# A macaron block on one core: the L1 mixtures in two per pass, one a sequence, with attention's key sums on TensorE and the RWKV set-up moved down

## The chip, the cores and the metric

The kernel runs on one core of one Trainium2 chip. The metric is device time in microseconds (us); lower is better. All arithmetic is in f32. The kernel before ran three times: 1630.42, 1637.78 and 1638.27 us, median 1637.78 us.

## The reference, cut to what matters

The input is two sequences of 1024 tokens with 256 features, 2048 tokens in all. Six residual steps follow each other, three of "layer 0" and three of "layer 1":

```
x = x + 0.5 * moe0(layernorm(x))      # 8 experts, the best 2 per token, hidden 176, and a shared part
x = x + rwkv(layernorm(x))            # a token needs the token before it
x = x + 0.5 * moe0(layernorm(x))      # same weights
x = x + 0.5 * moe1(layernorm(x))      # 32 experts, the best 6 per token, hidden 96, and a shared part
x = x + attention(layernorm(x))
x = x + 0.5 * moe1(layernorm(x))      # same weights
```

A mixture routes each token by a softmax (layer 0) or a sigmoid (layer 1) over its experts and adds the weighted outputs of `silu(x Wg) * (x Wu) Wd` of the chosen experts. The shared part is one more such network that all tokens go through. Nothing in a mixture ties one token to another.

The attention of layer 1 is linear. It works on one sequence:

```
Q, K, V = split(X @ W_in.T + b_in);   Q, K = rope(Q), rope(K)     # first 128 features turned
A = sum over tokens of (K / max(|K|, 1e-12)) * V                  # one vector of 256 per sequence
Y = (A * Q) @ W_out.T + b_out + X
```

So a token's output needs all tokens of its own sequence, and none of the other's.

## The kernel before, in words

**Tiles.** All of x stays in SBUF, as 16 tiles of 128 tokens; tiles 0 to 7 are the first sequence, 8 to 15 the second. The code calls eight tiles a half (`HT`), and four tiles a batch (`BT`).

**A mixture (`sparse_moe`, L311).** Its steps are generators, one for each of these:

- `ready(h)` (L674) for a half: `prep` (L339) normalizes a batch on VectorE, transposes it on TensorE (L123), multiplies it with the router (L354) and picks the experts (`route`, L133). `plan` (L377) ranks the tokens of each expert with three matmuls (L390 to L397) and gives every pair of token and expert a slot. Slots lie in blocks of 128, and a block belongs to one expert. `owners` (L469) lists each block's expert.
- `scatter(h)` (L450): GpSimd writes each normalized row to its slots in a DRAM buffer `xs`, with one indirect DMA for a tile and one choice: 16 for a half of layer 0, 48 for a half of layer 1.
- `shared(h)` (L542): the shared network, a tile at a time.
- `blocks()` (L656): for each block, SP fetches 128 slots (`fetch`, L569), TensorE transposes them (`features`, L580), multiplies with gate and up weights (`inner`, L593), ScalarE and VectorE form silu times up (L503, L504), TensorE turns that and multiplies it with the down weight (`outward`, L608), VectorE copies it out (L616), and SP stores it to a DRAM buffer `ys`. The four steps of neighbouring blocks are taken in turn, one of each per round. A fetch waits for all scatters issued so far.
- `combine(h)` (L645): GpSimd gathers each pair's row from `ys` (L627), VectorE adds it, weighted, to x (L638), four gathers behind.

The number of blocks is fixed beforehand, for the worst split of tokens over experts (`moe_blocks`, L40): 39 for layer 0 and 127 for layer 1. Slots of layer 1's second half that fit into blocks of the first are put there. A gather for the first half waits for the first 79 blocks (23 in layer 0), one for the second half for all blocks.

**The order of the work.** `play` and `side_by_side` (L272 to L308) run the generators beside each other. Each yields an engine and an assumed time; the one whose planned clock is lowest goes next. What comes out is a fixed order of instructions for TensorE, VectorE, ScalarE and SP (`ORDERED`). Each of these engines takes its instructions in that order and stands when one has to wait. GpSimd's order is set by the framework's own scheduler. `after` (L1014) holds a generator until named steps have been planned.

**The stages.** Loads of x, of layer 0's weights and a fill of `xs` with zeros open SP's queue; the ten small RWKV vectors and seven RWKV weights follow (`load_rwkv`, L700). There, five small VectorE operations form one minus a mixing vector (L708); they are the first that VectorE has to do after three set-up operations. Then come the first layer-0 mixture over all 16 tiles, RWKV in four batches, the second layer-0 mixture, the first layer-1 mixture over all 16 tiles, attention of the first sequence, routing of its tiles for the second layer-1 mixture, attention of the second sequence (`attend`, L869), routing, and the second layer-1 mixture over all 16 tiles, whose results are stored.

**Attention.** For each tile (`products`, L890) TensorE forms queries, keys and values, VectorE adds biases and turns queries and keys. In `sums` (L931) ScalarE squares the keys and sums them, VectorE adds the residual and the bias, takes the root's reciprocal for that tile, multiplies key, value and that number (L947) and adds it to an accumulator (L948). Two matmuls with a column of ones at the end sum over the partitions. `queries` (L950) transposes the queries. After the last tile the output weight is scaled by A, and the output matmuls follow.

Of the kernel before, what the change touches and what calls it, by code (L numbers as in the profile page):

```python
# [8 lines left out]
F32 = mybir.dt.float32  # L9
I32 = mybir.dt.int32  # L10
# [29 lines left out]
def moe_blocks(m):  # L40
    return (NTOK * m["K"] + m["E"] * (P - 1)) // P
# [3 lines left out]
def macaron_kernel(ctx: ExitStack, tc: tile.TileContext, a: dict, out: bass.AP):  # L45
# [58 lines left out]
    def normalize(src, dst, n, name):  # L104
# [9 lines left out]
        for i in range(n):  # L114
            nc.vector.tensor_scalar(  # L115
                dst[i], src[i], mv[:, i, 0:1], rstd[:, i : i + 1], ALU.subtract, ALU.mult
            )

# [68 lines left out]
    def sparse_tiles(pool, layer):  # L187
# [17 lines left out]
            blocks=moe_blocks(m),  # L205
# [49 lines left out]

    def fill_slots(xs, n, behind=None):

        zero = const.tile([P, D], F32, tag="zero", name=f"zero_{n}")
        nc.gpsimd.memset(zero, 0.0)
# [12 lines left out]
    def side_by_side(*parts):  # L272

        clocks, waits = [clock["now"]] * len(parts), [None] * len(parts)
        left = set(range(len(parts)))
        while left:
# [9 lines left out]
            n = min(able, key=lambda n: (clocks[n], n))  # L286
            if clocks[n] > clock["now"]:
                yield "until", clocks[n]
# [15 lines left out]
    def play(*parts):  # L304
        for step in side_by_side(*parts):
# [5 lines left out]
    def sparse_moe(layer, w, nth, xs, ys, moe, last=False):  # L311

        name = f"{layer}_{nth}"
        E, K, H, C, HP, NBLK = (w[k] for k in ("E", "K", "H", "C", "HP", "blocks"))
        SH, SU, rows = w["SH"], w["SU"], w["rows"]

        first = (HT * P * K + E * (P - 1)) // P
        xs, ys = xs[0 : NBLK * P, :], ys[0 : NBLK * P, :]
# [3 lines left out]
        def begin(h):  # L322
            nonlocal taken, comb, past, slot, top, idx, wk, who, ends
            if h == 0:
                taken = moe.tile([P, NT, E], F32, tag="taken", name=f"taken_{name}")
                comb = moe.tile([P, NT, E], F32, tag="comb", name=f"comb_{name}")
                past = moe.tile([P, NT + 1, E], F32, tag="past", name=f"past_{name}")
                slot = moe.tile([P, NT, E], F32, tag="slot", name=f"slot_{name}")
                top = back.tile([P, NT, 8], F32, tag="top", name=f"top_{name}")
                idx = back.tile([P, NT, K], I32, tag="idx", name=f"idx_{name}")  # L330
                wk = back.tile([P, NT, K], F32, tag="wk", name=f"wk_{name}")
                who = moe.tile([P, P], I32, tag="who", name=f"who_{name}", bufs=2)
                ends = moe.tile([P, 2, E], F32, tag="ends", name=f"ends_{name}")
# [5 lines left out]
        def prep(b):  # L339
# [4 lines left out]
            normalize(x[ts], xb, BT, sub)  # L344
# [850 lines left out]
```

## Time and profile before

| what | value |
|---|---|
| median of three runs | 1637.78 us |
| the profiled execution's own time | 1638.15 us |
| its span, first to last instruction | 1636.0 us |
| mean granted TensorE clock | 0.868 of full speed |
| TensorE busy | 1189.7 us, 73% |
| VectorE busy | 802.1 us, 49% |
| ScalarE busy | 559.6 us, 34% |
| GpSimd busy | 523.1 us, 32% |
| DMA | 203.06 MB, mean 124 GB/s |

Stages by the timeline, from the span's start: the first transposes of a mixture at 56.8 us, the first blocks of layer 0 at 158.5, RWKV's first transposes at 268.1 and its end at 490, layer 0's second blocks from 597.5 to 709.5, layer 1's blocks from 862 to 1069 and from 1347.9 to 1564. In the profile PE is TensorE, DVE VectorE, ACT ScalarE, POOL GpSimd and SP SyncE; a name such as `xb_L<-xs_L` is what an instruction writes and reads, with numbers left out. A waiting engine is listed with what ended the wait. Every matmul in f32 counts as two records, a transpose as one. The time of a TensorE record includes its way through the array, so neighbouring records overlap, and pace is read from the starts.

### The profile page before, as it was taken

The numbers are of one execution on the slowest core, as the hardware profiler recorded it, in microseconds if no ns is written. First come the engines' busy times: TensorE is split into PE (matmuls) and PEld (weight loads), VectorE is DVE, ScalarE is ACT, GpSimd is POOL, SyncE is SP. The second block draws the span as 40 slices with busy tenths as digits, with TensorE's granted clock in tenths as the row PEclk, the third lists the DMA queues.
The fourth block names the chain that finished last, engine by engine and source line by source line (L and its number), as shares of the span: only waits on it lengthen the run. The fifth ranks groups of instructions, "written<-read, shape, count | busy, mean of one in ns | idle before, by whom it ended". The sixth has DMA issues, their size and how long they took to land.

```text
span 1636.0 us, 21526 instructions
## 1 busy us (share of the span) xinstructions
PE 1189.7 (73%) x5462; PEld 888.9 (54%) x5462; DVE 802.1 (49%) x2588; ACT 559.6 (34%) x1551; POOL 523.1 (32%) x559
## 2 busy tenths in 40 slices
PE   0489997699996999876508998964685609998820
PEld 0366764366565777644307887743454408887610
DVE  0453346855515522556503445688776514445543
ACT  0142344576723333322104554420341104453310
POOL 0042034011113400337770005556271460005556
PEclk9999998799996999976758999987696759999965
DMA  9411343920008113464225557722020135557743
GB/s 276 119 58 63 100 143 93 331 77 1 0 0 210 56 56 107 133 169 140 103 103 151 172 174 224 237 88 81 32 103 26 62 106 158 172 172 217 226 120 105
DMA packets 182911, 203.06 MB, mean 124 GB/s; under 512 B 40044, under 2 KB 165772, under 8 KB 182796
## 3 DMA queue, kind: packets, MB, share of 16 engines
q1 hardware_dynamic: 158220, 134.55, 27.6%
q0 software_dynamic: 24576, 67.14, 13.3%
q8 instruction: 52, 0.85, 0.2%
q14 instruction: 63, 0.52, 0.1%
HBM read 100.68 MB, written 100.93 MB: 123 GB/s over the span
## 4 chain that ended last, share of the span: by engine, by line
PE 44%; DVE 13%; POOL 9%; DMA 8%; issue 7%; ACT 3%; POOLq 0%; ACTq 0%; DVEq 0%; SPq 0%
PE pg_L_b L593 12%; POOL xs_L L455 8%; PE py_L_b L608 7%; PE px_L L580 4%; DMA xb_L<-xs_L 4%; PE pkv_cm L761 3%; PE pkk_cm L749 3%; DMA yk_L<-ys_L,idx_L 3%; PE pg_L L513 3%; PE ph_L_b L529 2%; PE py_L L555 2%; DVE x L638 1%; PE lg_L L354 1%; PE po_at L761 1%; POOL yk_L L627 1%
## 5 line engine op out<-in xcount | busy, mean ns | idle before, releaser
L627 POOL DMA_INDIRECT yk_L<-ys_L,idx_L x256 | 248.8, 972 | 631.1 <-DMA ys_L<-yb_L 484.2
L455 POOL DMA_INDIRECT xs_L<-xn_L,idx_L x256 | 248.2, 970 | 263.4 <-DVE idx_L L446 77.7
L504 DVE TENSOR_TENSOR h_L_b<-g_L_b,pg_L_b 128x96 f32<-128x96 f32 (+1 forms) x332 | 90.6, 273 | 370.9 <-ACT g_L_b L503 370.4
L593 PE MATMUL pg_L_b<-L1gu,xbT_L 128*128 x1016 | 220.2, 341 | 21.0 <-ACT xbT_L L584 12.9
L584 ACT COPY xbT_L<-px_L 128x256 f32<-128x256 f32 x332 | 123.5, 373 | 279.0 <-PE px_L L580 276.8
L580 PE MATMUL px_L<-ident,xb_L 128*128 128x128 f32 x664 | 130.1, 278 | 108.6 <-DMA xb_L<-xs_L 108.2
L593 PEld LDWEIGHTS pg_L_b<-L1gu,xbT_L 128*128 128x128 f32 x1016 | 163.9, 195 | 36.0 <-issue 17.6
L580 PEld LDWEIGHTS px_L<-ident,xb_L 128*128 128x128 f32 x664 | 92.1, 143 | 151.0 <-DMA xb_L<-xs_L 97.9
L638 DVE SCALAR_TENSOR_TENSOR x<-yk_L,wk_L,x 128x256 f32<-128x256 f32 x256 | 121.3, 480 | 75.1 <-DMA yk_L<-ys_L,idx_L 73.5
L616 DVE COPY yb_L<-py_L_b 128x256 f32<-128x256 f32 x332 | 140.6, 424 | 29.4 <-PE py_L_b L608 27.3
L608 PE MATMUL py_L_b<-L1down,hT_L_b 96*128 x508 | 153.4, 383 | 0.2 <-ACT hT_L_b L536 0.2
L503 ACT ACTIVATE g_L_b<-pg_L_b 128x96 f32<-128x96 f32 (+1 forms) x332 | 88.6, 267 | 160.5 <-PE pg_L_b L593 159.4
L593 PE MATMUL pg_L_b<-L0gu,xbT_L 128*128 x312 | 107.0, 466 | 6.3 <-ACT xbT_L L584 5.5
L529 PE MATMUL ph_L_b<-ident,h_L_b 128*96 128x128 f32 (+1 forms) x410 | 100.3, 276 | 2.4 <-DVE h_L_b L504 2.2
L536 ACT COPY hT_L_b<-ph_L_b 96x128 f32<-96x128 f32 (+1 forms) x332 | 92.8, 280 | 3.6 <-PE ph_L_b L529 3.5
L513 PE MATMUL pg_L<-L0sgu,xTs_L 128*128 128x352 f32 x256 | 88.9, 497 | 0.0
L608 PEld LDWEIGHTS py_L_b<-L1down,hT_L_b 96*128 96x128 f32 x508 | 77.4, 193 | 10.3 <-ACT hT_L_b L536 0.9
L608 PE MATMUL py_L_b<-L0down,hT_L_b 88*128 x312 | 81.4, 384 | 1.0 <-ACT hT_L_b L536 1.0
L503 ACT ACTIVATE g_L<-pg_L 128x176 f32<-128x176 f32 (+1 forms) x96 | 29.8, 322 | 150.4 <-PE pg_L L513 150.2
L123 PE MATMUL pt_L<-ident,xn_L 128*128 128x128 f32 x128 | 28.6, 376 | 69.6 <-DVE xn_L L115 66.7
L504 DVE TENSOR_TENSOR h_L<-g_L,pg_L 128x176 f32<-128x176 f32 (+1 forms) x96 | 31.7, 341 | 72.1 <-ACT g_L L503 72.0
L593 PEld LDWEIGHTS pg_L_b<-L0gu,xbT_L 128*128 128x128 f32 x312 | 53.6, 191 | 24.3 <-ACT xbT_L L584 6.2
(216 smaller groups left out, 1823.0 us busy)
## 6 DMA issues: line engine op xcount, KB each, us to landing
xb_L<-xs_L SPq DMA_DIRECT2D x332, 128.0 KB
ys_L<-yb_L SPq DMA_DIRECT2D x332, 128.0 KB
xs_L<-zero SPq DMA_DIRECT2D x1, 16256.0 KB
xs_L<-zero SPq DMA_DIRECT2D x1, 4992.0 KB
xs_L<-xn_L,idx_L POOLq DMA_INDIRECT x256, 2.4
yk_L<-ys_L,idx_L POOLq DMA_INDIRECT x256, 3.1
L1gu<-in_L_gate SPq DMA_DIRECT2D x8, 384.0 KB
L1gu<-in_L_up SPq DMA_DIRECT2D x8, 384.0 KB
```

Of the source, the lines that this page charges most:

```text
L455: d = nc.gpsimd.indirect_dma_start(out=xs, out_offset=bass.IndirectOffsetOnAxis(ap=idx[:, t, k : k + 1], axis=0), in_=xn[h][:, i, :], in_o ...
L503: nc.scalar.activation(g, pg[:, 0:width], AF.Silu)
L504: nc.vector.tensor_tensor(dst, g, pg[:, width : 2 * width], ALU.mult)
L513: nc.tensor.matmul(pg, xT[half][:, c, i * P : (i + 1) * P], w["sgu"][:, c, u, :, :].rearrange("p z w -> p (z w)"), start=(c == 0), stop=(c ...
L529: nc.tensor.transpose(pt[0:m, k * P : (k + 1) * P], h[:, r : r + m], ident)
L580: nc.tensor.transpose(px[:, c * P : (c + 1) * P], xb[:, c * P : (c + 1) * P], ident)
L584: nc.scalar.copy(xbT.rearrange("p c t -> p (c t)"), px[:, 0 : DC * P])
L593: nc.tensor.matmul(pg, xbT[:, c, :], w["gu"][:, c, bass.ds(e, 1), :, :].rearrange("p e z h -> p (e z h)"), start=(c == 0), stop=(c == DC - 1),
L608: nc.tensor.matmul(py, hT[0:HP, k, :], w["down"][:, bass.ds(e, 1), k, :].rearrange("p e d -> p (e d)"), start=(k == 0), stop=(k == C - 1),)
L616: nc.vector.tensor_copy(yb, py)
L627: d = nc.gpsimd.indirect_dma_start(out=yk, out_offset=None, in_=ys[0 : n * P, :], in_offset=bass.IndirectOffsetOnAxis(ap=idx[:, t, k : k + ...
L638: added = nc.vector.scalar_tensor_tensor(x[t], gathered.pop((t, k)), wk[:, t, k : k + 1], x[t], ALU.mult, ALU.add)
```

## The change

**Mixtures of layer 1.** Each of the two passes is now two mixtures, one for each sequence, called A and B. Each has its own `xs` and `ys`, its own slots and its own 79 blocks (`moe_blocks(w, HT)`). Layer 0 stays one mixture over 16 tiles. The tiles with routing data get two buffers, and `zero` is set once.

**Order.** `prep` can wait for its batch (`behind`). The first pass plans A's scatter, blocks of A with B's routing and shared network among them, then blocks of B with A's gathers and the first sequence's attention among them. The second pass does the same, with A's blocks beside B's gathers and the second sequence's attention. A filler may be named in `play`: it goes on where the others would leave TensorE free for more than 0.5 us by the plan. The second shared pass of layer 0, and that of the last mixture, are fillers. The planned costs of some steps are new numbers.

**Attention.** Residual and bias go into one operation per tile in `norms`; the norm's root is taken once for all tiles; key times value stays in the tile of normalized features, and 16 matmuls with the column of reciprocal norms form A. Scratch data is put into PSUM banks.

**Set-up.** The five RWKV operations move from the head into `rest_of_mixing`, behind the first mixture.

```diff
-def moe_blocks(m):
-    return (NTOK * m["K"] + m["E"] * (P - 1)) // P
+def moe_blocks(m, tiles=NT):
+    return (tiles * P * m["K"] + m["E"] * (P - 1)) // P
...
+        parts = [*parts, *([filler] if filler is not None else [])]
...
+            if filler is not None and len(parts) - 1 in able:
+                others = [m for m in able if m != len(parts) - 1]
+                if others:
+                    n = min(others, key=lambda n: (clocks[n], n))
+                    if clocks[n] > max(free["PE"], clocks[-1]) + 0.5:
+                        n = len(parts) - 1
...
+    def sparse_moe(layer, w, name, first_tile, tiles, xs, ys, moe, last=False, behind=None):
...
+        NBLK = moe_blocks(w, tiles)
+        halves = tiles // HT
...
+            if behind is not None:
+                yield lambda: behind(b)
...
             if "_m" in v:
-                u = pool.tile([P, DC], F32, name=f"u_{v}")
-                nc.vector.tensor_scalar(u, t, -1.0, 1.0, ALU.mult, ALU.add)
-                rw[f"1-{v}"] = u
+                rw[f"1-{v}"] = pool.tile([P, DC], F32, name=f"u_{v}")
...
+    def rest_of_mixing():
+        for v in ("tm_mk", "tm_mv", "tm_mr", "cm_mk", "cm_mr"):
+            nc.vector.tensor_scalar(rw[f"1-{v}"], rw[v], -1.0, 1.0, ALU.mult, ALU.add)
...
+            minus[g] = small.tile([P, BT], F32, tag="minus", name=f"minus_{name}_{g}", bufs=4)
+            nc.vector.scalar_tensor_tensor(minus[g], mean, -1.0, rstd, ALU.mult, ALU.mult)
+            nc.vector.tensor_scalar(rstd, rstd, 1.0, None, ALU.add)
+            for i, xt in enumerate(xs[ts]):
+                nc.vector.scalar_tensor_tensor(
+                    xt, xt, rstd[:, i : i + 1], at["b_out"], ALU.mult, ALU.add
+                )
...
-            nc.vector.tensor_tensor(xs[t], xs[t], xl[:, t, :], ALU.add)
-            nc.vector.tensor_tensor(xs[t], xs[t], at["b_out"], ALU.add)
...
-                nc.vector.scalar_tensor_tensor(v, qk[:, 1, :], ss, v, ALU.mult, ALU.mult)
-                nc.vector.tensor_tensor(acc, acc, v, ALU.add)
...
+            nc.scalar.activation(
+                pv[:, D : 2 * D], qk[:, 1, :], AF.Square, accum_out=ss[:, t : t + 1]
+            )
+            nc.vector.tensor_tensor(v, v, qk[:, 1, :], ALU.mult)
...
+            for t in range(TPB):
+                nc.tensor.matmul(
+                    pA[:, c : c + 1],
+                    xl[:, t, c * P : (c + 1) * P],
+                    ss[:, t : t + 1],
+                    start=(t == 0),
+                    stop=(t == TPB - 1),
+                )
...
+                play(*mixture(m), filler=after([(d, "ready1")], m["shared"](1)))
+                rest_of_mixing()
...
+            after([(d1[0], "ready0")], m1[0]["scatter"](0)),
+            after([(d1[0], "scatter0"), (d0, "blocks")], m0["combine"](1)),
...
+            halfs_blocks(m1[0], [(d1[0], "shared0"), (d0, "blocks")]),
...
+            halfs_blocks(m1[1], [(d1[0], "nearly")]),
+
+            after([(d1[0], "first")], m1[0]["combine"](0)),
+            after([(d1[0], "first"), (d1[1], "shared0")], attention(0)),
+            after([(at, ("done", 0, 0))], m2[0]["ready"](0)),
+            after([(d2[0], "ready0"), (d1[0], "combine0")], m2[0]["scatter"](0)),
...
+            halfs_blocks(m2[0], [(d1[1], "nearly"), (d2[0], "shared0")]),
+            after([(d1[1], "first"), (d2[0], "scatter0")], m1[1]["combine"](0)),
+            after([(d1[1], "first"), (d2[0], "shared0")], attention(1)),
+            after([(at, ("done", 1, 0))], m2[1]["ready"](0)),
+            after([(d2[1], "ready0"), (d1[1], "combine0")], m2[1]["scatter"](0)),
+            halfs_blocks(m2[1], [(d2[0], "nearly")]),
+            after([(d2[0], "first"), (d2[1], "scatter0")], m2[0]["combine"](0)),
+            after([(d2[1], "blocks"), (d2[0], "combine0")], m2[1]["combine"](0)),
+            filler=fill(
+                after([(d0, "ready1")], m0["shared"](1)),
+                after([(d2[1], "ready0")], m2[1]["shared"](0)),
+            ),
```

## The prediction

> **What bounds the kernel now.** I cut the span into stages at points read from the timeline, then read the busy time of each engine in each stage; columns are the stretch, its length, busy us (records) per engine, granted TensorE clock, DMA share, GB/s.
>
> ```profile
> core 0: us, PE busy (x) PEld busy (x) DVE busy (x) ACT busy (x) POOL busy (x), PEclk, DMA share, GB/s
> 0.00:56.80 56.80, 0.00 (x0) 0.00 (x0) 4.07 (x19) 1.58 (x2) 2.06 (x15) 1.00 0.90 252
> ...
> 709.50:861.00 151.50, 63.22 (x223) 43.92 (x222) 64.92 (x241) 17.63 (x43) 108.42 (x112) 0.64 0.45 137
> 861.00:988.00 127.00, 120.78 (x726) 105.36 (x727) 53.42 (x158) 62.65 (x243) 0.00 (x0) 0.97 0.56 168
> 988.00:1069.00 81.00, 73.13 (x419) 59.24 (x417) 50.41 (x143) 36.73 (x140) 46.54 (x48) 1.00 0.77 226
> 1069.00:1174.60 105.60, 60.01 (x194) 39.48 (x194) 85.94 (x287) 16.01 (x49) 47.43 (x48) 0.74 0.22 63
> 1174.60:1347.00 172.40, 89.61 (x340) 62.56 (x340) 92.51 (x314) 38.43 (x90) 93.68 (x96) 0.72 0.21 74
> 1347.00:1474.00 127.00, 121.31 (x728) 105.05 (x728) 53.99 (x160) 62.84 (x244) 0.00 (x0) 0.98 0.56 168
> 1474.00:1564.00 90.00, 76.64 (x413) 62.31 (x413) 49.40 (x140) 35.62 (x138) 45.59 (x48) 0.94 0.71 212
> 1564.00:1636.00 72.00, 0.70 (x2) 0.30 (x2) 24.79 (x52) 0.03 (x1) 45.42 (x48) 0.53 0.39 110
> ```
>
> In the stages of L1 blocks (861 to 1069, 1347 to 1564) TensorE is busy 85% to 96%: it bounds them. Elsewhere another thing does. From 709.5 to 861 GpSimd is busy 108 of 151 us: its indirect row moves (248.8 us for 256 gathers, 248.2 for 256 scatters, one each 1.265 us by the starts below). From 1069 to 1347, attention and the second routing, TensorE is busy 150 of 278 us at a clock of 0.72 to 0.74. The last 72 us are gathers alone.
>
> The waits, longest first (engine, tile, line, releaser: total, times, longest):
>
> ```profile
> PE px_L L580 <- DMA xb_L<-xs_L: 108.2, 19, 55.1
> ...
> DVE u_tm_mk L708 <- DMA v_tm_mk<-in_tm_mk: 48.2, 1, 48.2
> ...
> POOL zero L259 <- DMA xs_L<-zero: 28.0, 1, 28.0
> ```
>
> VectorE stands 48.2 us before its first real work, for a vector of the RWKV set-up queued behind all L0 weights. TensorE waits twice, 55.1 us the longest, for the first slots of a pass.
>
> The timeline of GpSimd before the second L1 pass:
>
> ```profile
> 1283.56 0.96 POOL L455 DMA_INDIRECT xs_L<-xn_L,idx_L  x1 [47.21 <-DVE passed_L L472]
> ...
> 1343.19 0.96 POOL L455 DMA_INDIRECT xs_L<-xn_L,idx_L  x1 [0.30 <-issue]
> ```
>
> 48 scatters take 60.9 us; the last lands 2.4 us later, and the first transposes of the blocks start at 1347.85. From that pass's ranking on TensorE (1274.4) to its first block: 73 us.
>
> TensorE where L1's normalization already stands among L0's blocks:
>
> ```profile
> 685.39 0.38 PE L580 MATMUL px_L<-ident,xb_L 128*128 128x128 f32 x2
> ...
> 690.79 2.72 PE L593 MATMUL pg_L_b<-L0gu,xbT_L 128*128 x4 [5.02 <-ACT xbT_L L584]
> ```
>
> The blocks halt 5.0 us behind a ScalarE copy, which stood behind a Sqrt that waited for VectorE.
>
> **The change, part by part.** Times are on the trace's clock. The profiled execution was 1638.15 us around a span of 1636.0; the median is 1637.78, so I add 2 us at the end. For places I use the order in which the changed program's instructions stand on each engine.
>
> *Start.* The five set-up operations leave the head of VectorE's queue; they go behind the mixture, where 5 x 0.17 us cost 1 us. The loads moved no place in SP's queue. By 10.5 us the DMA has moved 2.1 MB (estimate from its rate there, 182 to 301 GB/s), which is the first eight x tiles plus router and shared weights. Normalizing tiles 4 to 7 started at 57.6 and the first scatter at 79.45, 21.9 us later; from 10, that is 32. The zero fill ended by 30.35 (GpSimd waited for it until then), so it holds nothing. Gain 47; if loads come late, 30.
>
> *L0 mixtures.* The second shared pass is now a filler: 69 of the 160 matmuls stand behind the blocks, 6.9 tiles x 4.0 us (pace at 567 to 591) = 27.6. First mixture: second plan 35 us after the first scatter (before: 39, one tile more ahead of it), 16 scatters 20.2, landing and fetch 4.5: blocks at 92 instead of 158.5. Then +27.6 behind them: 39 us ahead. RWKV's start gap of 7.7 us shrinks to about 4, and its adds find their rows landed (2 us): 44 ahead when RWKV ends. Second mixture: the same move makes scatters (573 + 2.4), not shared work (595), set the blocks' start: 22.5 earlier, 66.5 in all. Its deferred shared work now stands under the next wait.
>
> *First L1 block.* Before, 96 scatters of both sequences had to land; now 48. L0's blocks end at 643; slots are ready about 13 us later; on GpSimd eight gathers stand ahead of the scatters and wait for L0's last store, and from the blocks' end to the first scatter it was 16.5 us (709.5 to 726), so 660; 48 scatters 60.7; landing and fetch 4.5: 725 instead of 861. TensorE's 24 + 19 us of shared work fit in the wait. The two fills write 20.7 MB instead of 16.6, some 12 us more at 331 GB/s, in the RWKV stage, where the DMA then idles from 360 to 480: nothing; 12 without that cover. **136 us ahead**; bounds 115 and 150.
>
> *More blocks.* A pass had 127 blocks, now 79 + 79: 62 more in all. A clean pass of 79 with filling took 127 us (861 to 988; 1.53 a block after filling), so they cost about 95 us, and none lies beside a wait, for TensorE bounds there.
>
> *What moves among the blocks.* By TensorE's pace at full clock: a shared pass 8 x 2.38 = 19 us (732.2 to 734.6); 16 transposes at 0.11 (a block's two take 0.22), router 2 x 1.8 (699.5 to 701.3), ranking 1.7, in all 7; attention 8 x (1.72 + 0.86 products, 4 x 0.11 transposes, 0.87 output) + 32 records of the sums at 0.11, in all 35. The sums take the place of two ones-matmuls a sequence. On VectorE a tile's burst is now 0.68 + 0.41 + 0.57 + 3 x 0.43 = 2.95, with 0.44 in the normalization; it was 4.58 in all. That saving lies under TensorE, which bounds, so it is worth nothing by itself.
>
> VectorE and ScalarE are in order, so each such burst holds block work behind it, and then TensorE. The row: from the transposes at 685.39 to the next at 695.72 is 10.3 us, less 0.9 of other transposes, against 2.5 for such a block: two normalizations cost 7 us; L1's shorter blocks have less slack: 8. A routing blocks VectorE 6.2 us (698.8 to 705.0), of which its matmuls and a block cover 4: 2 each. The plan is 7 us on VectorE, 4 uncovered; slot weights 2. Attention's normalization is 6.7 us (four more operations of 0.44), 5 uncovered, twice. An attention tile has no row inside blocks: from 0 (its 2.6 us of matmuls cover the burst) to 4; I take 0.75, as the two nearly match; the tail 3. So 18 us of halts in the first mixed stage, and 13 + 10 + 6 + 3 = 32 in each with an attention; bounds 5 and 30, 8 and 65.
>
> Here a rule speaks against the change. The row: a table load takes 1.28 us, and the Silu after the load at 690.76 starts at 692.05, with nothing between. The Trainium skill (ScalarE: Activation LUTs, What ACT_TABLE_LOAD costs) adds a drain of about 1.38 us to every switch. The order has 6, 14 and 14 loads inside the three mixed stages. By the row they are in my halts; by the rule 34 x 1.38 = 47 us more, an estimate. I take the row.
>
> *Gathers beside blocks.* 48 blocks beside 48 gathers took 81 us, and 90 where output stores joined, against 73.4 clean: +8 a stage, +15 in the last. A scatter beside blocks is not seen; from 0 to 12, I take 3, since it brings no adds.
>
> *L1 in sequence.* First sequence: 127 + 19 + 7 + 18 + 3 = 174, to 899. Second sequence with attention 0: 79 x 1.53 = 121, less 5 because diluted fetches wait less (1.42 us pace at 1060 to 1064), + 8 + 35 + 7 + 32 = 198, to 1097. Second pass, first sequence: its ranking stands behind all but the last of those 79 blocks, since all of attention precedes it, and SP's fetches wait for its scatters: **73 us in which only 19 us of shared work is left**, to 1170. Blocks with attention 1: 127 - 5 + 8 + 35 + 7 + 32 = 204, to 1374. Again 73, less 3 for two blocks behind the ranking: 1444. Blocks: 127 + 15 = 142, to 1586. Gathers of all 48 rows: 72, to 1658. Before, this part took 775 us; now 933.
>
> Against each other: 136 ahead at the front, 158 behind after it: **+22 us, 1658 + 2 = 1660**.
>
> **Rivals.**
> *Smooth interleaving (faster).* Bursts hide fully, gathers cost nothing and diluted blocks run at 1.42: mixed stages of 156, 154 and 160 us: 106 less, 1554. It decides once the three together fall more than 30 us below my 576. For it: VectorE has some 145 us of work in about 200. Against: the halt above, and gathers that cost 8 to 17.
> *VectorE paces the mixed stages.* Tiles with adds (6 us of VectorE beside 6 of TensorE) and PSUM banks held through the rotation cost 4 us a tile: +26 in each of two stages, and 10 for longer normalizations: 1722.
> *The start is not gained.* Fill, loads and scatters collide: 17 us lost, 1677.
> *Clock.* Work that ran at 0.72 should run at 1.00. The Trainium skill (TensorE: Matmul & The Clock Gate, What's actually happening) has idle of some 3.4 us halve the clock. If halts keep it at the 0.72 row, attention's 35 us become 49 a sequence: 1688. I take full clock: dense stages show 0.97 to 1.00.
>
> **How the numbers follow.** Forecast, with late start and slow clock inside its own range 1625 to 1705: 0.62. Smooth: 0.22, 1554 to 1625. VectorE pacing: 0.16, above 1705. The 80% range is 1590 to 1730. A measurement tells about 0.5%, 8 us: faster is below 1630, smooth and a little of the forecast, 0.24; same, to 1646, 0.12; slower 0.64.
>
> **What would show it.** First scatter near 32; first L1 block near 725; two waits of TensorE for first slots, 45 to 55 us, ahead of the second pass's stages; clock 1.0 in mixed stages, and these near 174, 198 and 204; last gathers 72. Wrong if mixed stages fall under 180, or if a second-pass scatter runs beside blocks.

## The result

The changed kernel takes 1693.14 us (median of four, 1688.74 to 1700.46) against 1637.38: a ratio of 1.0355, 95% interval 1.0308 to 1.0401. It is slower, as forecast, but by 56 us and not by 22. The forecast's own range ended at 1705, so the place is inside it; the size of the loss is two and a half times what the sum had.

The stages of the changed kernel (stretch, length, busy us and records per engine, granted TensorE clock, DMA share, GB/s):

```profile
core 0: us, PE busy (x) PEld busy (x) DVE busy (x) ACT busy (x) POOL busy (x), PEclk, DMA share, GB/s
0.00:32.40 32.40, 16.69 (x61) 13.87 (x62) 17.97 (x106) 7.03 (x11) 1.77 (x15) 1.00 0.93 286
...
726.50:902.80 176.30, 152.57 (x847) 127.78 (x847) 89.64 (x310) 76.84 (x267) 50.95 (x55) 0.93 0.51 160
902.80:1125.00 222.20, 184.43 (x925) 147.49 (x925) 124.57 (x391) 88.42 (x290) 47.22 (x48) 0.90 0.41 120
1125.00:1194.00 69.00, 22.01 (x83) 14.87 (x83) 18.21 (x64) 5.18 (x16) 48.97 (x51) 0.68 0.30 102
1194.00:1419.00 225.00, 185.18 (x925) 148.35 (x925) 128.92 (x418) 88.46 (x290) 46.23 (x48) 0.89 0.40 119
1419.00:1480.10 61.10, 22.45 (x84) 14.93 (x83) 14.01 (x38) 5.18 (x16) 46.47 (x49) 0.67 0.33 112
1480.10:1621.60 141.50, 126.30 (x711) 105.13 (x711) 73.42 (x207) 61.33 (x237) 43.34 (x46) 0.95 0.65 194
1621.60:1692.60 71.00, 0.02 (x1) 0.00 (x0) 23.66 (x49) 0.00 (x0) 45.37 (x48) 0.52 0.38 108
```

Set beside the forecast's places, almost every line fits:

| step | forecast | measured |
|---|---|---|
| first scatter | 32 | 32.4 |
| first blocks of layer 0 | 92 | 91.3 |
| first block of layer 1 | 725 | 726.5 |
| first sequence, first pass | 174 | 176.3 |
| second sequence, first pass, with attention 0 | 198 | 222.2 |
| to the next block | 73 | 69.0 |
| first sequence, second pass, with attention 1 | 204 | 225.0 |
| to the next block | 70 | 61.1 |
| second sequence, second pass | 142 | 141.5 |
| last gathers | 72 | 71.0 |
| end of the span | 1658 | 1692.6 |

The two stages that hold an attention are 45 us longer than forecast; the stretches to the next block are 13 us shorter, 4 at the first and 9 at the second: from each ranking on they take 72 and 71 us instead of 73, and 2.7 and 9.8 us of block work stand behind the ranking, where next to nothing and 3 had been counted. That is all of the miss but some 2 us.

The starts that answer to the first scatter, the first slots and the second pass's scatters (timeline, GpSimd and TensorE):

```profile
32.38 1.15 POOL L468 DMA_INDIRECT xs_L<-xn_L,idx_L  x1 [30.05 <-DVE idx_L L459]
...
726.47 0.69 PE L595 MATMUL px_L_0A<-ident,xb_L_0A 128*128 128x128 f32 x2 [31.01 <-DMA xb_L_0A<-xs_A]
...
1129.78 1.00 POOL L468 DMA_INDIRECT xs_A<-xn_L_1A,idx_L_1A  x1 [136.29 <-DVE idx_L_1A L459]
```

The waits (engine, tile, line, releaser: total us, times, longest):

```profile
PE px_L_1B L595 <- DMA xb_L_1B<-xs_B: 43.4, 10, 37.4
PE px_L_1A L595 <- DMA xb_L_1A<-xs_A: 43.2, 3, 41.3
...
PE px_L_0A L595 <- DMA xb_L_0A<-xs_A: 33.0, 5, 31.0
```

VectorE's 48.2 us for `u_tm_mk` are gone from this list, as is GpSimd's wait for the zero fill. TensorE waits for first slots three times; 41.3 and 37.4 stand ahead of the second pass's stages, where 45 to 55 were named. The first scatter of the second pass (1129.78) starts 5 us after the last block of the stage ahead of it, so nothing hides it. For the second sequence the first scatter (1415.88) comes 3.3 us before the last block's end (1419.17): three scatters of 48 run beside blocks, which by its letter is one of the forecast's signs of being wrong, though 57 us of scatters stay exposed.

Now the stage from 1194 to 1419. TensorE stands 39.8 us in it (225.00 - 185.18); the forecast had 32 of halts and 8 for gathers, 40. What the forecast did not have is in the last columns: a granted clock of 0.89. The trace lists that clock as stretches of either 1.0 or 0.5. TensorE was busy for 44.9 us inside stretches of 0.5, which at full clock are 22.4: 22.4 us lost. The work at full clock is then 185.2 - 22.4 = 162.8 us, and the forecast had 204 - 40 = 164. So the sums of work and of halts were right, and the clock is the difference. In the stage before it, the same sum gives 37.8 of halts, 41.2 busy at half clock (20.6 lost) and 163.8 of work, 6 more than forecast.

Three stretches around the second normalization of attention 0 show how that comes about:

```profile
core 0: us, PE busy (x) PEld busy (x) DVE busy (x) ACT busy (x) POOL busy (x), PEclk, DMA share, GB/s
1002.80:1009.50 6.70, 4.35 (x26) 3.46 (x24) 5.65 (x20) 4.14 (x10) 0.00 (x0) 1.00 0.41 121
1009.50:1016.40 6.90, 4.65 (x16) 3.97 (x17) 3.72 (x13) 1.97 (x9) 0.00 (x0) 0.51 0.20 64
1016.40:1023.20 6.80, 6.80 (x39) 5.45 (x38) 2.70 (x8) 2.47 (x8) 0.00 (x0) 1.00 0.42 130
```

VectorE is busy with the burst in the first line and TensorE halts (busy 4.35 of 6.70). In the second line the clock is at one half for 6.8 us: TensorE is busy 4.65 us for 16 records, 0.29 us each, where in the third, at full clock, 39 records take 6.80 us, 0.17 each.

And the halt of an attention tile, on ScalarE:

```profile
1027.06 0.25 ACT L550 COPY hT_L_0B_b<-ph_L_0B_b 96x128 f32<-96x128 f32 x1
1032.01 0.39 ACT L961 ACTIVATE pav_at<-qk_at 128x256 f32<-128x256 f32 x1 [4.70 <-DVE qk_at L959]
1032.34 0.19 ACT L961 ACTIVATION_READ_ACCUMULATOR pav_at<-qk_at 128x1 f32 x1
1032.43 0.35 ACT L974 COPY axT_at<-pqT_at 128x256 f32<-128x256 f32 x1
1032.68 0.37 ACT L599 COPY xbT_L_0B<-px_L_0B 128x256 f32<-128x256 f32 x1
```

ScalarE stands 4.70 us before the square of the keys, which needs the turned keys from VectorE. The block's copies (L599) stand behind it. TensorE's next transposes wait 0.94 us for the square itself (listed as `px <- pav_at`), and the gate matmuls another 0.45 behind the copies. I had put the halt of an attention tile down to VectorE's burst, at 0.75 us; most of it is ScalarE's order. The kernel before had the square one step later, behind the next tile's products; the change moved it up.

### The profile page after: what moved, and what is told of

The parts are those of the page before. It is cut to its first block, busy times and chain, and to the rows that moved or that the text cites. A ratio compares the mean times of both kernels' runs of the same rounds, so it can differ in the third digit from the quotient of the medians.

```text
span 1692.6 us, 23886 instructions
## 1 busy us (share of the span) xinstructions
PE 1301.3 (77%) x6080; PEld 986.5 (58%) x6080; DVE 823.0 (49%) x2658; ACT 626.1 (37%) x1740; POOL 519.4 (31%) x558
## 4 chain that ended last, share of the span: by engine, by line
PE 54%; DVE 14%; POOL 11%; DMA 8%; issue 8%; ACT 4%; SPq 0%; ACTq 0%; POOLq 0%; DVEq 0%
PE pg_L_b L608 5%; POOL xs_A L468 5%; PE py_L_b L623 4%; PE pkv_cm L783 3%; PE pg_L_0A_b L608 3%; PE pkk_cm L771 3%; PE pg_L_1B_b L608 3%; POOL xs_B L468 3%; PE pg_L_1A_b L608 3%; PE pg_L_0B_b L608 2%; PE pg_L L527 2%; DMA xb_L_1B<-xs_B 2%; PE pqk_at L926 2%; PE py_L_0A_b L623 2%; DMA yk_L_1B<-ys_B,idx_L_1B 2%
## 5 line engine op out<-in xcount | busy, mean ns | idle before, releaser
L642 POOL DMA_INDIRECT yk_L<-ys_L,idx_L x64 | 61.6, 962 | 217.5 <-DMA ys_L<-yb_L 143.4
L608 PE MATMUL pg_L_b<-L0gu,xbT_L 128*128 x312 | 111.5, 482 | 6.8 <-ACT xbT_L L599 6.8
L468 POOL DMA_INDIRECT xs_L<-xn_L,idx_L x64 | 61.7, 964 | 106.2 <-DVE h_L L518 33.5
L608 PE MATMUL pg_L_0B_b<-L1gu,xbT_L_0B 128*128 x316 | 74.5, 363 | 13.8 <-ACT xbT_L_0B L599 7.8
L608 PE MATMUL pg_L_1A_b<-L1gu,xbT_L_1A 128*128 x316 | 74.9, 364 | 12.4 <-ACT xbT_L_1A L599 7.6
L608 PE MATMUL pg_L_0A_b<-L1gu,xbT_L_0A 128*128 x316 | 70.7, 349 | 8.8 <-ACT xbT_L_0A L599 7.8
L608 PE MATMUL pg_L_1B_b<-L1gu,xbT_L_1B 128*128 x316 | 70.1, 346 | 6.9 <-ACT xbT_L_1B L599 3.3
L608 PEld LDWEIGHTS pg_L_b<-L0gu,xbT_L 128*128 128x128 f32 x312 | 55.7, 199 | 25.8 <-ACT xbT_L L599 7.8
L608 PEld LDWEIGHTS pg_L_0B_b<-L1gu,xbT_L_0B 128*128 128x128 f32 x316 | 55.7, 210 | 19.9 <-ACT xbT_L_0B L599 9.3
L595 PE MATMUL px_L_1B<-ident,xb_L_1B 128*128 128x128 f32 x158 | 31.9, 286 | 43.4 <-DMA xb_L_1B<-xs_B 43.4
L771 PE MATMUL pkk_cm<-mk_cm,w_WkeyT 128*128 128x512 f32 x128 | 60.5, 610 | 4.7 <-DVE mk_cm L762 3.8
```

The costliest lines, as they stand in the source:

```text
L468: d = nc.gpsimd.indirect_dma_start(out=xs, out_offset=bass.IndirectOffsetOnAxis(ap=idx[:, t, k : k + 1], axis=0), in_=xn[h][:, i, :], in_o ...
L595: nc.tensor.transpose(px[:, c * P : (c + 1) * P], xb[:, c * P : (c + 1) * P], ident)
L608: nc.tensor.matmul(pg, xbT[:, c, :], w["gu"][:, c, bass.ds(e, 1), :, :].rearrange("p e z h -> p (e z h)"), start=(c == 0), stop=(c == DC - 1),
L642: d = nc.gpsimd.indirect_dma_start(out=yk, out_offset=None, in_=ys[0 : n * P, :], in_offset=bass.IndirectOffsetOnAxis(ap=idx[:, t, k : k + ...
L771: nc.tensor.matmul(ps, w[:, c, oc * P : (oc + 1) * P], src[:, c, :], start=(c == 0), stop=(c == DC - 1),)
```

## The experiments

Some runs fell on chips where the engines stood up to 15 us at a time while rows were being scattered, and where the kernel before took 1845 to 1849 us; I call these the held-up chips. Such runs are compared as ratios to the kernel before on the same chip, or in the stage of second-pass blocks of the first sequence, which has next to no scatter in it and took 226.0 us there against 225.0. The changed kernel ran on one held-up chip of three (ratio 1.0265) and on one free chip of two; runs from the others are set against these. The other runs are from free chips, where the kernel before took 1637; their differences are of medians, and those of the ratios are 2 to 6 us smaller. Where one edit ran on both, the two expectations follow each other.

### The start alone

```diff
-                u = pool.tile([P, DC], F32, name=f"u_{v}")
-                nc.vector.tensor_scalar(u, t, -1.0, 1.0, ALU.mult, ALU.add)
+                rw[f"1-{v}"] = pool.tile([P, DC], F32, name=f"u_{v}")
...
+                rest_of_mixing()
```

> The kernel before with one edit: the five RWKV operations behind the first mixture. The forecast's start step: first scatter near 32 us instead of 79, and 47 us less at the end, since the rest of the order is that of before: 1590. Rival (loads, fill and scatters collide): first scatter near 50, 30 us less: 1607.

Measured (held-up): 1801.57 against 1846.73, ratio 0.9755 (0.9722 to 0.9789), 45 us less; first scatter at 31.8. The 47 of the forecast's start step stand, on a held-up chip.

### Layer 1 in one mixture again

```diff
-    for k, layer, tiles in (("L0", "L0", NT), ("A", "L1", HT), ("B", "L1", HT)):
+    for k, layer, tiles in (("L0", "L0", NT), ("L1", "L1", NT)):
...
+    m1 = sparse_moe("L1", w1, "L1_0", 0, NT, xs["L1"], ys["L1"], moe_pool)
+    m2 = sparse_moe("L1", w1, "L1_1", 0, NT, xs["L1"], ys["L1"], moe_pool, last=True)
...
+            after([(d1, "combine0"), (d1, "blocks")], attention(0)),
+            after([(at, ("done", 0, 1))], m2["ready"](0)),
```

> The changed kernel with layer 1 put back into one mixture of 16 tiles and 127 blocks per pass, attention between the passes; start, filler and the new attention stay. If the split is what costs: the front keeps 66 us, attention's shorter VectorE bursts bring 10 to 25 between the passes: 1545 to 1565. If the new attention (sums on TensorE, longer normalization) is what costs: 1600 or more.

> Layer 1 in one mixture of 127 blocks per pass, beside the changed kernel on the same chip. The split costs what the forecast's sum has for it, corrected by what was measured: 62 blocks at 1.5 us and the exposed scatters, against 70 us of an earlier first block: 100 to 125 us below the changed kernel.

> The changed kernel again, as the measure for the two runs beside it: its stage of second-pass blocks of the first sequence 225 us long.

Measured: ratio 0.9649 (0.9618 to 0.968) on a held-up chip, above the 0.943 to 0.956 that 1545 to 1565 would be. Beside the changed kernel on a free one: 1565.82 us, ratio to before 0.955 (0.9517 to 0.9584), against 1692.70 (1.0312, 1.0265 to 1.0359) for the changed kernel: 127 us less, a little more than the 100 to 125 expected. The timeline of the one-pass kernel by stages:

```profile
core 0: us, PE busy (x) PEld busy (x) DVE busy (x) ACT busy (x) POOL busy (x), PEclk, DMA share, GB/s
798.40:1007.20 208.80, 194.35 (x1143) 164.31 (x1143) 104.09 (x300) 99.34 (x382) 46.66 (x48) 0.98 0.63 189
1007.20:1284.00 276.80, 164.56 (x590) 114.76 (x590) 167.66 (x550) 42.72 (x117) 139.41 (x144) 0.71 0.21 71
1284.00:1495.00 211.00, 196.71 (x1143) 166.81 (x1143) 103.87 (x300) 98.63 (x381) 45.82 (x48) 0.97 0.63 191
```

Its first block of layer 1 comes at 798.4, 67 us after the changed kernel's 731.7; from there to the end it takes 767.9 us, the changed kernel 959.7. So the split brings 67 at the front (the forecast has 69.5 for it: 136 less the 66.5 of start and filler) and costs 192 behind it (forecast 158). The stage between the passes, with the new attention, takes 276.8 us against 278 before (1069 to 1347): the new attention as a whole, with less work on VectorE for a tile, a longer normalization and the earlier square, is worth next to nothing there. With start, filler and new attention alone, and layer 1 left whole, the kernel is 72 us faster than before.

### Fewer blocks

```diff
+        LIVE = NBLK - 11 if E == 32 else NBLK
...
-            for q in range(-lead, NBLK + 4):
+            for q in range(-lead, LIVE + 4):
```

> The changed kernel with 68 blocks instead of 79 in each of the four layer-1 mixtures, so 44 blocks less; the last 11 blocks are not computed, their rows get copies of other blocks' rows. The forecast's price of 1.53 us a block, with nothing to hide them: 67 us less than the changed kernel. Rival (blocks fill halts that would be there anyway): 30 us or less.

Measured (held-up): ratio 0.9909 (0.9884 to 0.9933); the changed kernel on such a chip had 1.0265, so 0.0356 x 1849 = 66 us less for 44 blocks, 1.50 a block (some 0.2 either way by the two intervals). The mean price of the extra blocks stands, and most of it shows. It is not even, though: the four block stages get 15, 29, 23 and 13 us shorter, and the two exposed stretches 9 and 6 us longer, since the rankings now stand behind the last block there. What a single block costs is not shown by this run.

### Idle matmuls in the halts

```diff
+            for _ in range(cold["n"]):
+                nc.tensor.matmul(
+                    px[:, DC * P : DC * P + P], every, ident, start=True, stop=True
+                )
+            cold["n"] = 0
```

> The changed kernel with idle matmuls added in the first block round behind each layer-1 normalization (12 of 128x128) and each attention normalization (20), where TensorE halts anyway. Clock theory: the half-speed stretches behind those bursts (about 20 us of 40 in each stage with an attention, 10 in the first mixed stage) vanish, TensorE's records shorten: 10 us less in each of the two stages, 4 in the first, 1670. Rival (VectorE's bursts pace the stage, the clock is a by-product): no change, or up to 8 us more, 1693 to 1701.

> The changed kernel with 16 idle matmuls of 128x128 in the first block round behind each layer-1 normalization and 26 behind each attention normalization. Clock theory: the half-speed stretches behind these bursts go (20 us a stage with an attention, half of that lost time), 15 to 25 us below the changed kernel. Rival (VectorE's bursts pace the stage): 0 to 8 us above it.

> The changed kernel itself, as the measure for the three runs beside it. Every theory expects the ratio to before of 1.03 to 1.04, unless slots and rows land later on this chip.

Measured (held-up): 1891.64 (ratio 1.0222, 1.0176 to 1.0267) with the fewer idle matmuls, 1890.73 (1.0247, 1.0205 to 1.029) with the more, and 1895.69 (1.0265, 1.0221 to 1.031) for the changed kernel beside the second. Both stayed between the theories. The stage of 226.0 us tells why. It is 224.7 long with the idle matmuls; TensorE stands 29.4 us instead of 41.0, and of its busy time 25.7 instead of 42.0 is at half clock, 8.1 us regained. The two together are 19.7; the 84 idle matmuls of this stage take 0.22 us each, 18.5. Half speed lasts 26.7 us in this stage instead of 51.9: with halts filled the clock stays up. But what a busy TensorE wins back, the matmuls that keep it busy take away.

### The square of the keys one step later

```diff
-            nc.scalar.activation(
-                pv[:, D : 2 * D], qk[:, 1, :], AF.Square, accum_out=ss[:, t : t + 1]
-            )
...
+        def queries(t, both):
+            qk, pv = both
             nc.scalar.activation(
                 pv[:, D : 2 * D], qk[:, 1, :], AF.Square, accum_out=ss[:, t : t + 1]
             )
...
+            if t >= 1:
+                queries(*done)
             if t < TPB:
                 qk = products(t)
-            if t >= 1:
-                queries(*done)
```

> The changed kernel with the square of the keys issued one step later, so that ScalarE does not stand before it with block copies behind. If ScalarE's stand is the halt of an attention tile (1.4 us of TensorE a tile in the trace of after), 16 tiles give 15 to 25 us less. Rival (VectorE's work for the tile is the limit): within 5 us of the changed kernel.

Measured (held-up): 1872.83, ratio 1.0157 (1.0114 to 1.0199), 23 us below the changed kernel beside it. In the stage of 226.0 us, now 217.5, TensorE stands 31.9 us instead of 41.0, while 44.5 us at half clock are left: this takes halts away and leaves the clock as it was (42.0 at half clock without the edit). The edit also puts the last tile's queries ahead of the next products; the two parts did not run apart, but the wait for the square, 7.7 us there, is gone.

In the one-pass kernel, where no blocks lie between attention's tiles, the same edit does not help:

> Layer 1 in one mixture of 127 blocks per pass, with the start, the filler and the new attention of the changed kernel, and the late square. Attention stands between the passes here, where ScalarE's stand is on the path: 5 to 15 us below the one-pass kernel (whose ratio to before was 0.965), so 0.957 to 0.962. If TensorE or VectorE sets the pace of those tiles: 0.965.

Measured (held-up): ratio 0.9697 (0.9668 to 0.9727), a miss. The products of attention 0's eight tiles span 54.5 us there (1140.6 to 1195.1) against 45.2 (1138.8 to 1184.0): the transposes of the last tile's queries now stand ahead of the next tile's products on TensorE, and without blocks between them they come before VectorE has turned those queries. That last reason is argued from the order, not tried.

### The key sums of before

```diff
-            nc.scalar.activation(
-                pv[:, D : 2 * D], qk[:, 1, :], AF.Square, accum_out=ss[:, t : t + 1]
-            )
...
+            nc.scalar.activation(pv[:, D : 2 * D], qk[:, 1, :], AF.Square, accum_out=s1)
+            nc.vector.tensor_scalar(s1, s1, 1e-24, None, ALU.max)
+            nc.scalar.activation(s1, s1, AF.Sqrt)
+            nc.vector.reciprocal(s1, s1)
...
+                nc.vector.scalar_tensor_tensor(v, qk[:, 1, :], s1, v, ALU.mult, ALU.mult)
+                nc.vector.tensor_tensor(acc, acc, v, ALU.add)
...
+            sums(t, qk, pv)
```

> The changed kernel with the key sums of before: a root, a reciprocal, a weighting and an addition per tile on VectorE and ScalarE, and two one-column matmuls at the end in place of 16. Forecast's view: 1.5 us more of VectorE per tile, of which about 1 shows, 16 tiles: 10 to 20 us above the changed kernel, in spite of the 4 us of one-column matmuls saved per sequence. [...] Rival (the clock lost behind the one-column matmuls, 10 us at half speed each, outweighs this): 0 to 10 us below it.

Measured (held-up): 1891.29, ratio 1.0226 (1.0167 to 1.0285), 4 us below the changed kernel with intervals that overlap, where 10 to 20 above were expected: a miss. But the edit has two parts. With the sums, the square also goes behind the next tile's products, where the kernel before had it, and a later square alone brought 23 us. In the stage of 226.0 us (226.2 here) the 7.7 us that TensorE waits for the square are gone, and 10.4 us behind ScalarE's copies have come, while ScalarE stands 26.0 us for the roots. Against the late square on the same chip this run is 18 us slower. So the forecast's price for the old sums may well be right; the sums alone, with the square left where it is, did not run.

The run has 128 table loads against 100, and for the same reason its time says little about them. The trace says more. In the changed kernel's trace (ScalarE) the next function starts when the load ends:

```profile
1099.76 1.28 ACT L517 ACT_TABLE_LOAD   x1
1101.06 0.25 ACT L517 ACTIVATE g_L_0B_b<-pg_L_0B_b 128x96 f32<-128x96 f32 x1
```

1099.76 + 1.28 is 1101.04. In the median of the 100 loads the next function starts 0.01 us behind the load's end. No drain is seen, and the forecast was right to take the row.

### Normalizations a tile at a time

```diff
+        for i in range(n):
+            nc.vector.bn_stats(st, src[i])
+            nc.vector.bn_aggr(mv[:, i, :], st)
+            yield "DVE", 1.0
...
-                norms(t // BT)
-                yield "DVE", 5.5
+                yield from norms(t // BT)
```

> The changed kernel with the normalizations a tile at a time and nothing else. If bursts and the clock behind them are a cause of their own, the stages with an attention shrink from 225 to some 208, the half-speed share with them, and the whole gains 25 to 40 us. If ScalarE's stand before the square was the whole cause and the bursts only looked like one, the stages stay within 5 us of 225.

> The changed kernel with the late square and, in addition, with the layer-1 and attention normalizations issued a tile at a time among the blocks instead of four tiles in one burst. Clock theory: no halt over 1 us is left at the normalizations, so the half-speed stretches behind them go (4 of 8 in a stage), and the second sequence's first pass and the second pass's first shrink by more than the idle time that goes: some 15 us a stage from first block to last against the late square alone. As the ranking moves behind the last block in this order, the whole gains less: 0 to 20 us under the late square. Rival (VectorE's total work is the limit): stages as with the late square alone.

> The changed kernel with late square and normalizations a tile at a time, the ranking behind the last block: 1635 to 1645, that is 50 to 60 below the changed kernel, with both stages with an attention at 195 to 203 us from first to last block, which is the forecast's 198 and 204.

Measured: the split of the bursts alone 1663.23 (ratio 1.0146, 1.0099 to 1.0193), 29 us below the changed kernel beside it, as expected. With the late square 0.9941 (0.9921 to 0.996) on a held-up chip, 40 us below the late square alone where up to 20 were expected, and 1647.98 (1.0077, 1.0054 to 1.0099) on a free one: 45 us below the changed kernel, a little less than the 50 to 60 expected. The same stage, from first to last block, in the changed kernel as it ran beside the split bursts, with the split bursts, and with both edits (columns as above):

```profile
1195.60:1420.30 224.70, 185.50 (x925) 148.42 (x925) 128.99 (x418) 88.61 (x290) 46.23 (x48) 0.88 0.40 119
```

```profile
1179.10:1375.10 196.00, 172.74 (x919) 139.72 (x919) 115.61 (x366) 87.99 (x290) 35.38 (x38) 0.95 0.44 130
```

```profile
1169.80:1358.50 188.70, 173.27 (x919) 140.15 (x919) 114.45 (x366) 90.35 (x290) 35.60 (x38) 0.95 0.45 135
```

| stage with attention 1 | length | TensorE stands | busy | of it at half clock | work at full clock |
|---|---|---|---|---|---|
| forecast | 204 | 40 | 164 | 0 | 164 |
| changed kernel | 224.7 | 39.2 | 185.5 | 44.7 | 163.2 |
| late square (held-up chip) | 217.5 | 31.9 | 185.6 | 44.5 | 163.4 |
| bursts split | 196.0 | 23.3 | 172.7 | 20.3 | 162.6 |
| both | 188.7 | 15.4 | 173.3 | 19.9 | 163.4 |

The work is the same 163 us in every measured row. The late square removes halts alone (on its chip the changed kernel stands 41.0 and has 42.0 at half clock). The split bursts remove 16 us of halts and, with the same edit, 12 us of lost clock. A small part of that has only moved out of the stage: the ranking now stands behind the last block, and in the changed kernel the 10.3 us from the ranking on hold 3.3 us of halts and 3.1 busy at half clock. The halts by releaser, in the changed kernel, with the split bursts alone and with both edits (that stage, TensorE):

```profile
PE ph_L_1A_b L543 <- DVE h_L_1A_b L518: 14.7, 8, 2.8
PE pg_L_1A_b L608 <- ACT xbT_L_1A L599: 9.8, 9, 2.0
PE px_L_1A L595 <- ACT pav_at L961: 7.8, 8, 1.2
```

```profile
PE px_L_1A L624 <- ACT pav_at L996: 7.7, 8, 1.2
PE ph_L_1A_b L572 <- DVE h_L_1A_b L547: 5.6, 4, 2.8
...
PE pg_L_1A_b L637 <- ACT xbT_L_1A L628: 1.7, 4, 0.6
```

```profile
PE ph_L_1A_b L572 <- DVE h_L_1A_b L547: 4.8, 4, 2.8
...
PE pg_L_1A_b L637 <- ACT xbT_L_1A L628: 0.8, 3, 0.5
```

In the first block, the first line is what stands behind VectorE's bursts. The second is in the main the same cause: its three longest halts, 2.0 us each, stand behind a root on ScalarE that waits for VectorE's statistics, and the split alone takes it to 1.7. The third is the square: the split leaves it at 7.7, and with both edits it is gone. With both edits these stages take 189.4 and 188.7 us, less than the forecast's 198 and 204. The whole gains less than the stages do (32 and 36), because in this order the ranking slips behind the last block: from its start to the next stage's first block it is 74.6 and 79.3 us instead of 71.8 and 71.5, and all of it is exposed.

### The ranking earlier

```diff
+    def quick(part):
+        for step in part:
+            yield step if callable(step) or step[0] == "until" else (step[0], 0.33 * step[1])
...
-            after([(d1[0], "first"), (d1[1], "shared0")], attention(0)),
+            quick(after([(d1[0], "first"), (d1[1], "shared0")], attention(0))),
```

> The changed kernel, where attention, the next normalizations, routing and ranking are planned at a third of their cost, so that they come closer together among the blocks: the ranking of a second-pass sequence stands 14 blocks before the end instead of behind the last one. If the place of the ranking sets the exposed scatters: the two waits of TensorE shrink by about 20 us each, less some 5 for denser bursts: 1660. Rival (denser bursts hold the blocks by as much as they bring): 1685 to 1700.

> The changed kernel with attention, routing and ranking planned at a third of their cost, the ranking 14 blocks earlier; on a chip where the kernel before takes 1640 the scatters run beside the blocks as in the first mixed stage. If the exposed scatters follow the ranking's place: waits of TensorE ahead of the second pass's stages below 25 us each instead of 41 and 37, 40 to 60 us below the changed kernel: 1635 to 1655. Rival (what is exposed less comes back as halts of the blocks): 1675 or more.

Measured: ratio 1.0114 (1.0079 to 1.0149) on a held-up chip, and 1636.35 us (0.9993, 0.9978 to 1.0009) on a free one: 56 us below the changed kernel, level with before and within what was expected. Its waits for first slots, and its first scatter of the second pass:

```profile
PE px_L_1A L595 <- DMA xb_L_1A<-xs_A: 25.7, 6, 22.3
PE px_L_1B L595 <- DMA xb_L_1B<-xs_B: 19.4, 8, 14.4
```

```profile
1102.70 1.00 POOL L468 DMA_INDIRECT xs_A<-xn_L_1A,idx_L_1A  x1 [108.58 <-DVE h_L_0B_b L518]
```

The scatters start 28 us before the stage's last block (1130.4) instead of 5 us behind it, and the next stage's first block comes at 1166.9 instead of 1195.6. From the ranking to that block it is 71.3 us as before; only what lies beside it is new. The exposed scatters follow the ranking's place.

All three edits together:

> The changed kernel with the late square, normalizations a tile at a time, and attention, routing and ranking planned at a third of their cost. If the exposed scatters follow the ranking's place and the halts follow the bursts, the gains add: 23 us of the late square, 28 of the earlier ranking, some 10 of the bursts, 55 to 65 below the changed kernel. Rival (they are the same time counted twice): 30 to 40.

> The changed kernel with late square, normalizations a tile at a time and the earlier ranking together. If the three losses are separate: 20 to 25 for the square, 29 for the bursts, 40 to 60 for the ranking: 1580 to 1605, still above the one-pass kernel's 1566. If they are partly the same time: 1605 to 1640.

Measured: 1.0033 (1.0003 to 1.0064) on a held-up chip, and 1631.97 us (0.997, 0.9952 to 0.9988) on a free one, only 4 us below the earlier ranking alone, with intervals that overlap. They do not add. The stages with an attention are back at 219.0 and 217.9 us, with 29.2 and 32.0 of halts and 37 us at half clock in each. The likely reason is that steps which had been spread over rounds stand close together again when they are planned at a third; that was not tried apart. An order that has both, spread steps and an early ranking, was not found here.

## Why the prediction was right in sign and wrong in size

- *Start, layer-0 filler, first block of layer 1.* Right within 2 us at each place, and tried alone (45 for 47).
- *More blocks.* Right in the mean: 1.50 us a block for 1.53, unevenly spread.
- *Exposed scatters.* Right in cause: 73 and 70 named, 72 and 71 from the ranking on. The block work behind the second ranking was under-counted (9.8 us for 3). TensorE's waits are 41 and 37, not 45 to 55, also because it stands 5.7 us for the plan before its shared work in the first stretch.
- *First mixed stage and last stage.* 176.3 for 174, 141.5 for 142. The first has 23.7 us of standing, 9.7 of lost clock and 142.9 of work. The row of 127 us that its sum starts from (861 to 988) holds 6.2 of standing, 3.1 of lost clock and 117.7 of work; with these and the 18 + 3, the forecast has 30.3 for standing and clock together, against 33.4, and 143.7 of work. Right in its parts too, within 3 us.
- *Stages with an attention.* Here it failed, and the step is the clock: "I take full clock: dense stages show 0.97 to 1.00." Its sign, a clock of 1.0 in the mixed stages, read 0.93, 0.90 and 0.89. The rows used were of stages with few halts (6.2 us in 127). The clock stood among the rivals, but as a price on attention's own 35 us of work; it falls on whatever TensorE does in the microseconds behind a halt, blocks above all, and cost 20.6 and 22.4 us. Sum of the halts: 40 forecast, 37.8 and 39.8 measured. The forecast's own row had the sign: the four gate matmuls behind the halt of 5.02 us take 2.72 us (690.79), and the next four (695.94), which it does not show, half of that:

```profile
695.94 1.35 PE L593 MATMUL pg_L_b<-L0gu,xbT_L 128*128 x4
```

- *Inside the halts* the parts were off against each other, so that the good sum is in part luck. Behind bursts, and roots that wait for them, TensorE stands about 23 us in the second stage for 13 + 10 (the 13 has no working of its own). An attention tile was given 0.75 us for VectorE's burst, but ScalarE's stand before the square costs 1.1 a tile by the late square (9.1 us in eight tiles). For fetches it stands 1.9 us; the gathers were given 8, part of which may lie in the bursts.
- *Table loads.* Right to follow the row.
- *VectorE as pace-setter.* It would have shown as more standing time; there was none beyond the 40.
- *Smooth interleaving.* Not what this order does, nor what the other orders came to: with two edits the stages run at 189, and the work at full clock alone, 163.8 and 162.8 us, is more than its 154 and 160.

The total by terms: +20.6 and +22.4 for the clock, +6 of work in the first of the two stages, -13 for the blocks behind the rankings, -2.4 of halts, and about +1 elsewhere: 34.6, the distance from 1658 to 1692.6. Set against the contents of the 127 us row, the clock is +17.5 and +19.3 in these two stages, work +4.1 and +3.1, and standing +2.6 and -1.4: the sum had taken 11 us of filling and fetch waits off the first of them where the row has 6.2, and the work was a little under-counted. The clock stays by far the largest term.

## What to carry to other kernels

When steps with a burst on VectorE or a waiting instruction on ScalarE are laid among TensorE's work, price each twice: the halt, and the clock behind it (here 21 and 22 us of lost clock for 38 and 40 of halts). Spread such a step over rounds, and try an instruction that waits for another engine one step later: among blocks it brought 23 us, without blocks it did not help. And before work is made overlappable by splitting it, count what the split adds on the engine that bounds (62 blocks, 93 us at the measured 1.50) and what still stands in a row at the seams (70 us each): the overlap has to bring more than that.

## What the runs showed of the hardware that was not expected

The granted clock goes to one half behind far shorter halts than I had assumed. The trace changes it on a grid of 3.41 us. In the changed kernel from 700 us on, I took for every change to half speed TensorE's busy share in the 3.41 us before it: in all 25 cases it was 53% or less, in most of them 30% to 53%. The 173 windows at full speed that were followed by full speed had 52% or more, all but one at least 54%. So 1.6 us of standing inside one window was enough here, and filling the halts with idle matmuls kept the clock up. The split is not as clean everywhere: before 700 us, two of 12 changes follow windows busy 70% and 100%, and with both edits two of 14 follow 60% and 81%. The Trainium skill (TensorE: Matmul & The Clock Gate, What's actually happening) has the half clock follow an idle window of some 3.4 us; in these traces a half-busy one does it.

Sums with one-column matmuls seem to count for less than their busy time. At both attentions a halt of 1.70 us, before the 32 records of `pA_at`, starts half speed as elsewhere. But the next two windows are busy throughout by the records, `pA_at` first, and the clock stays at half in both, 10.2 us in all; after 700 us every other window at half speed that was busy throughout was followed by full speed.

On the held-up chips other engines stand while rows are scattered. In the changed kernel there the first mixed stage takes 234 us instead of 176. While the second sequence's rows are scattered, the timeline and the waits of that run have:

```profile
866.00:946.00 80.00, 28.07 (x104) 20.18 (x103) 11.96 (x51) 8.61 (x32) 46.13 (x48) 0.62 0.33 110
```

```profile
DVE h_L_0A_b L518 <- issue: 23.3, 3, 15.4
...
PE pg_L_0A_b L608 <- issue: 16.2, 2, 14.7
```

TensorE is busy 28 of 80 us, where a free chip has 59 of 62 beside the same scatters, and VectorE and TensorE stand 15 us at a time for nothing that the trace names. One of the two DMA queues that load instructions (q8) also has no load from 868.5 to 945.6 us; whether that is the cause, or only follows from TensorE's standing, stays open.
